# Cross-attention with one matrix for query and key, and the query's constant summed on VectorE

## The chip, the cores and the metric

The kernel runs on one core of a Trainium2 chip. The metric is device time in microseconds (us) of one execution. Of the kernel before, six executions are known.

## What is computed

One pre-norm decoder layer over `x` of 16 sequences x 128 tokens x 256 channels, with a context `ctx_1024` of the same shape, all in float32:

```python
x = x + attn(_layernorm(x), ...)                       # differential attention, 16 heads
x = x + xattn(_layernorm(x), ctx_1024, ctx_1024, ...)  # cross-attention, one head of 256
x = x + ffn(_layernorm(x), ...)                        # 16 routed experts (2 a token) and a shared one

def xattn(q, k, v, Wq, bq, Wk, bk, Wv, bv, Wf, bf):
    qp = q @ Wq.T + bq
    kp = k @ Wk.T + bk
    vp = v @ Wv.T + bv
    attn = softmax((qp / 8.0) @ kp.T)
    return gelu((attn @ vp) @ Wf.T + bf) + v
```

Only the cross-attention is touched by the change.

## The kernel before

A tile holds 128 tokens, that is one sequence, on the 128 partitions. Sequences are numbered by `b` (or `k`), and four of them make a group `g` (512 tokens). The four matrices of the cross-attention come in transposed, `xw["q"]` as `[input, output]`.

**The attention** runs as a software pipeline over the steps `k = 0..20`. Sequence `b` has its score maxima at step `b`, its probabilities at `b + 2`, the two halves of its weighted sum after that (`weigh`, `averaged`), the difference of its two softmaxes at `b + 3`, its RMS norm in `scales` (sum on VectorE, a power on GpSimd, L378, 2.9 us) and `normed` (a product on GpSimd, `o`, L385), and at `b + 5` it is turned on TensorE (`output_turned`, tile `pot`, L394) and projected (`output`, tile `py`, L403). Steps 16 to 20 have no new sequence and only drain the pipeline.

**The cross-attention** is dealt out over the last steps by hand: the dictionary `plan` names for a step `k` and a place 0 to 3 in it the functions that are issued there. What remains of groups 2 and 3 stands in a straight list after the loop, mixed with the layer norms and the routing of the experts and with `next(shared)`, which issues one piece of the shared expert (eight matmul records of 512 columns, 3.44 us). For a group `g` the functions are, in order: `cross_stats` and `cross_normed` (layer norm on VectorE), `turned` (sixteen TensorE transposes: the contexts into `cT`, the normed tokens into `xnT`; and an addition on GpSimd, L661), `queries` and `keys` (the two projections, eight matmul records each, L668; the queries leave PSUM through VectorE at L673, the keys through ScalarE at L678), `softmax` (scores `psc`, L689; their maximum, L694; four exponentials with a sum, L698), `probs_by_key` (`ppt`, L709), `mixes` (`pc`, L718), `finishes` (`pf`, L731; left through VectorE at L737) and `gelu` (with an addition on GpSimd, L746). The value and output weights are made into one matrix beforehand, in `value_weights_turned` and `value_weights`.

**What sets the order.** `in_order` pins the instructions of TensorE, VectorE, ScalarE and GpSimd to the order of the text, each engine for itself. So an engine that waits holds up everything behind it in the text. All PSUM tiles come from one pool of eight banks, in turn: the ninth tile after another waits until the other has been read.

After the cross-attention the router's choice is computed on VectorE (L1035 to L1128), GpSimd scatters the tokens to the experts' slots (`xd`, L1134, 32 indirect DMAs), TensorE goes on with the shared expert meanwhile, and then 36 tiles of routed tokens follow, back to back on TensorE, and at the end the gathers (L1199).

Of the kernel before, what the change touches and what calls it, by code (L numbers as in the profile page):

```python
# [9 lines left out]
F32 = mybir.dt.float32  # L10
AF = mybir.ActivationFunctionType
ALU = mybir.AluOpType
# [7 lines left out]
GB = 4  # L20
# [23 lines left out]
def tile_decoder(  # L44
# [148 lines left out]
    def load(out, in_):  # L193
        pin(nc.sync.dma_start(out=out, in_=in_))
# [7 lines left out]
    with actx:  # L202
# [361 lines left out]

        class cross:
# [19 lines left out]
        def cross_rest():  # L585
            cross.pr = s_tile([P, 3, GB, P], "k30", "x_pr")
            cross.rest, cross.taken = s_tile([P, 16 * D], "qb0", "x_rest"), 0
            cross.cT, cross.mixT = part([P, NC_, GT]), part([P, NC_, GT])
            cross.wv, cross.wvf = part([P, NC_, D]), part([P, NC_, D])
            cross.bvb, cross.bf = part([P, NC_, P]), part([P, D])  # L590
            cross.bq, cross.bk, cross.bv = part([P, NC_]), part([P, NC_]), part([P, NC_])

        def cross_weights():
# [13 lines left out]
            load(out=cross.bf, in_=bf.partition_broadcast(P))  # L607

# [54 lines left out]
        def projected(w, from_t):  # L663
            dst = share.tile([P, NC_, GT], F32, tag=f"{w}T", name=f"{w}T")
            for e in range(NC_):
                pp = bank([P, GT], "pp")
                for c in range(NC_):
                    nc.tensor.matmul(  # L668
                        pp, lhsT=cross.xw[w][:, c, e * P : (e + 1) * P], rhs=from_t[:, c, :],
                        start=(c == 0), stop=(c == NC_ - 1),  # L670
                    )
                if w == "q":
                    nc.vector.tensor_scalar(  # L673
                        dst[:, e, :], pp, cross.bq[:, e : e + 1], 1.0 / TEMPERATURE,
                        ALU.add, ALU.mult,
                    )
                else:
                    nc.scalar.activation(  # L678
                        dst[:, e, :], pp, AF.Identity, bias=cross.bk[:, e : e + 1]
                    )  # L680
            return dst

        def scored(g, qT, kT):
# [9 lines left out]
            nmax = share.tile([P, GB], F32, tag="nmax", name="nmax")  # L693
            nc.vector.tensor_reduce(nmax, psc, AX.X, ALU.max, negate=True)  # L694
            pr = cross.pr[:, g % 2]
            den = share.tile([P, GB], F32, tag="den", name="den")
            for b in range(GB):
                nc.scalar.activation(  # L698
                    pr[:, b, :], psc[:, b, :], AF.Exp, bias=nmax[:, b : b + 1],
# [4 lines left out]
            return pr, rec  # L704
# [43 lines left out]
        def queries(g):  # L748
            cross.qT = projected("q", cross.xnT)

        def keys(g):
            cross.kT = projected("k", cross.cT)

        def softmax(g):
            soft[g] = scored(g, cross.qT, cross.kT)

# [6 lines left out]
        def finishes(g):  # L763
# [17 lines left out]
            (18, 2): [(keys, 1)],  # L781
            (18, 3): [(finishes, 0), (softmax, 1)],
# [3 lines left out]
            (20, 0): [(keys, 2)],  # L786
            (20, 1): [(cross_stats, 3), (finishes, 1), (softmax, 2), (cross_normed, 3)],
# [199 lines left out]
    with sctx:  # L987
# [8 lines left out]
        keys(3)  # L996
# [320 lines left out]
```

## Time and profile before

| | us |
|---|---|
| median of six executions | 632.16 |
| lowest and highest | 628.21, 632.74 |
| the profiled execution: its own time | 631.2 |
| the profiled execution: its span | 629.5 |

The profile shows one execution. PE is TensorE's matmul side, PEld its weight loads, DVE is VectorE, ACT is ScalarE, POOL is GpSimd; L668 is line 668 of the kernel before. A row of a timeline has the start in us from the span's start, the time from the first start to the last end in us, the engine, the line and the operation, and in brackets how long the engine had been idle before and what ended that. One float32 matmul is two records in the trace, one transpose is one. The end of a matmul record is modelled, so the pace of TensorE is read from start to start: 0.43 us for a record of 512 columns, 0.215 us for one of 256, 0.107 us for one of 128 or of 16. PEclk is the clock that TensorE was granted, 1.00 being full speed.

In this execution the cross-attention's first projection starts at 223.3 us, its last piece on TensorE ends at 335.9 us, the scatter runs from 381.8 to 422.5 us, and the routed tiles from 452.9 us.

### The profile page before, as it was taken

What the parts mean: (1) busy time and instruction counts of PE and PEld (TensorE: products, weight loads), DVE (VectorE), ACT (ScalarE), POOL (GpSimd) and SP (SyncE); (2) the same over time, 40 slices, a digit from 0 to 9 for tenths busy, and PEclk for the clock granted to TensorE, in tenths of its full rate; (3) what the DMA queues carried; (4) which work ended last, traced back from release to release, by engine and by line L of the source; (5) the groups of instructions that cost most, each with busy time, mean ns of one, the idle gap of its engine ahead of it and who ended that gap; (6) DMA issues with size and microseconds to landing.
All of it is one profiled execution on the core that took longest, in us unless ns stands there. A gap on an engine that the chain in (4) does not pass through costs nothing. (4 is left out here: it accounts for less than half of the span.)

```text
span 629.5 us, 10681 instructions
## 1 busy us (share of the span) xinstructions
PE 571.8 (91%) x3836; PEld 382.9 (61%) x3836; DVE 304.6 (48%) x694; ACT 211.5 (34%) x476; POOL 182.4 (29%) x159
## 2 busy tenths in 40 slices
PE   2499999999998999988999999648899999999986
PEld 2254564564555656666666674335389999988445
DVE  7683785685677683634545336001132323220543
ACT  2034564665554556243464211000122222220110
POOL 5520062344233442551211005760000000004653
PEclk9589999999998999999999999959999999999999
DMA  3022352421104020005002501220299898812333
GB/s 117 15 95 87 101 208 105 186 102 35 70 3 137 4 77 1 2 0 183 18 2 80 188 0 68 103 97 1 76 329 276 270 286 273 251 43 77 108 109 117
DMA packets 59191, 67.63 MB, mean 107 GB/s; under 512 B 8576, under 2 KB 52096, under 8 KB 59136
## 3 DMA queue, kind: packets, MB, share of 16 engines
q1 hardware_dynamic: 55408, 57.21, 28.0%
q0 software_dynamic: 3072, 8.39, 4.2%
q10 hardware_dynamic: 656, 1.31, 0.6%
q8 instruction: 32, 0.52, 0.3%
q14 instruction: 23, 0.19, 0.1%
HBM read 41.73 MB, written 18.61 MB: 96 GB/s over the span
## 5 line engine op out<-in xcount | busy, mean ns | idle before, releaser
L298 DVE TENSOR_REDUCE nm<-pq 128x4 f32<-128x512 f32 x128 | 79.5, 683 | 42.8 <-PE pq L293 42.7
L1199 POOL DMA_INDIRECT yg<-yd,si x32 | 31.2, 974 | 166.2 <-issue 154.8
L962 PE MATMUL py<-w,h 128*128 128x256 f32 x256 | 59.9, 394 | 17.5 <-DVE h L954 14.3
L330 ACT ACTIVATE pr<-pk 128x384 f32<-128x384 f32 (+1 forms) x192 | 71.5, 463 | 12.5 <-PE pk L324 12.2
L1172 PE MATMUL pu<-xrT,w 128*128 128x128 f32 x576 | 70.2, 275 | 0.0
L1172 PEld LDWEIGHTS pu<-xrT,w 128*128 128x128 f32 x576 | 67.3, 192 | 0.1
L962 PEld LDWEIGHTS py<-w,h 128*128 128x128 f32 x256 | 50.5, 198 | 27.6 <-DVE h L954 15.5
L378 POOL TENSOR_TENSOR rms<-rms,mhalf 128x16 f32<-128x16 f32 x16 | 46.4, 2898 | 64.7 <-DVE rms L377 64.7
L954 DVE TENSOR_TENSOR h<-act,pb 128x512 f32<-128x512 f32 x32 | 21.9, 687 | 87.0 <-PE pb L948 41.2
L953 ACT ACTIVATE act<-pa 128x512 f32<-128x512 f32 x32 | 19.1, 597 | 126.9 <-PE pa L948 87.1
L948 PE MATMUL pa<-xT,w 128*128 128x512 f32 x128 | 60.4, 594 | 0.0
L948 PE MATMUL pb<-xT,w 128*128 128x512 f32 x128 | 60.1, 592 | 0.0
L1179 DVE TENSOR_TENSOR hT<-ract,pu 128x256 f32<-128x256 f32 x36 | 15.2, 421 | 63.8 <-ACT ract L1177 63.8
L324 PE MATMUL pk<-qb,k 32*128 32x384 f32 (+1 forms) x384 | 44.7, 505 | 0.0
L293 PE MATMUL pq<-kb,qT 32*128 32x512 f32 x256 | 44.1, 621 | 0.4 <-DVE a L359 0.4
L1134 POOL DMA_INDIRECT xd<-xn,si x32 | 31.2, 974 | 44.7 <-DVE si L1107 35.2
L948 PEld LDWEIGHTS pb<-xT,w 128*128 128x128 f32 x128 | 24.3, 190 | 30.6 <-issue 30.4
L948 PEld LDWEIGHTS pa<-xT,w 128*128 128x128 f32 x128 | 23.7, 190 | 24.6 <-issue 23.9
L1185 PE MATMUL pyr<-w,hT 128*128 x144 | 37.0, 380 | 0.0
L246 PE MATMUL pp<-xnT,wqk 128*128 128x512 f32 (+1 forms) x64 | 33.9, 655 | 2.3 <-DVE xnT L159 1.4
L341 PE MATMUL po<-pr,v 128*32 128x128 f32 x1024 | 35.5, 280 | 0.0
L1177 ACT ACTIVATE ract<-pu 128x256 f32<-128x256 f32 x36 | 13.8, 384 | 60.1 <-PE pu L1172 60.1
(175 smaller groups left out, 793.8 us busy)
## 6 DMA issues: line engine op xcount, KB each, us to landing
w<-in_L_ffn_routed_w_dram SPq DMA_DIRECT2D x88, 256.0 KB
xd<-zeros SPq DMA_DIRECT2D x11, 512.0 KB
xr<-xd SPq DMA_DIRECT2D x36, 128.0 KB
yd<-yr SPq DMA_DIRECT2D x36, 128.0 KB
w<-in_L_ffn_shared_w_dram SPq DMA_DIRECT2D x12, 256.0 KB
k<-kT SPq DMA_DIRECT2D x32, 64.0 KB
ctx<-in_ctx_dram SPq DMA_DIRECT2D x4, 512.0 KB
x<-in_x_dram SPq DMA_DIRECT2D x3, 512.0 KB
```

The costliest lines, as they stand in the source:

```text
L246: nc.tensor.matmul(pp, lhsT=wqk[:, c, n, e * P : (e + 1) * P], rhs=xnT[:, c, at:], start=(c == 0), stop=(c == NC_ - 1),)
L293: nc.tensor.matmul(pq, lhsT=qT[rows, c, i * P : (i + 1) * P], rhs=kbs[g % 2][rows, c, :, i * P : (i + 1) * P], start=True, stop=True,)
L298: nc.vector.tensor_reduce(nm[:, NM * t + 4 * c : NM * t + 4 * c + 4], pq, AX.X, ALU.max, negate=True)
L324: nc.tensor.matmul(pk, lhsT=k3s[g % 2][rows, k, i * P : (i + 1) * P], rhs=qbs[g % 2][rows, heads, i * P : (i + 1) * P], start=True, stop=True,
L330: nc.scalar.activation(pr[:, 0:n, :], pk, AF.Exp)
L341: nc.tensor.matmul(po[32 * t : 32 * t + 32, j, :], lhsT=vs[g % 2][:, i, 4 * t + j, :], rhs=prs[k][t][:, r, :], start=True, stop=True,)
L378: nc.gpsimd.tensor_tensor(rms, rms, mhalf.to_broadcast([P, H]), ALU.pow)
L948: nc.tensor.matmul(pp, lhsT=w[:, c, fs], rhs=xT[g][:, c, :], start=(c == 0), stop=(c == NC_ - 1),)
L962: nc.tensor.matmul(py[:, i, :], lhsT=hs[u][:, f, b * P : (b + 1) * P], rhs=units[u][2][:, f, :], start=(u == 0 and f == 0), stop=(u == NS ...
L1134: i = nc.gpsimd.indirect_dma_start(out=xd[:, :], out_offset=bass.IndirectOffsetOnAxis(ap=slots[n][:, t : t + 1], axis=0), in_=xns[t // GB] ...
L1172: nc.tensor.matmul(pu[:, n, f, :], lhsT=w12[:, c, n, f * P : (f + 1) * P], rhs=xrT[:, c, :], start=(c == 0), stop=(c == NC_ - 1),)
L1185: nc.tensor.matmul(py, lhsT=hT[:, f, :], rhs=w3[:, bass.ds(e * NC_ + f, 1), :], start=(f == 0), stop=(f == NC_ - 1),)
```

## The change

The scores are `(Wq x + bq) . (Wk c + bk) / 8`. The kernel after multiplies the matrices first: with `Wqk = Wq^T Wk` and `u = Wk^T bq` the part that depends on the context is `(Wqk^T x + u) . c / 8`, so that the scores are taken on the turned contexts `cT` and no keys are projected. What is left, `(x . Wq^T bk + bq . bk) / 8`, is one number for each query; it is computed as a product and sum on VectorE (`cross.same`) and subtracted from the shift of the softmax and added to it again.

- `query_weights_turned` (new, place (15, 3)): eight transposes of `Wq` and `Wk`, two ScalarE evictions of 512 columns, two VectorE products that spread `bk`.
- `query_weights` (new, (16, 1)): the product of the matrices (four matmuls of 256 columns), `u` (four of one column), the vector for the constant (two of 256 columns and two of one), and their evictions.
- `queries` uses `Wqk` and, beside the two evictions, issues four products with a sum over 256 channels and one small addition on VectorE. `queries(0)` and `cross_normed(1)` move from (15, 3) to (16, 3), where `keys(0)` stood.
- `keys` is gone for all four groups. `softmax` of group 1 moves to (18, 2), that of group 2 to (20, 0), that of group 3 to the place of `keys(3)`; `next(shared)` is shifted twice in the list after the loop. `softmax` has two more small operations on VectorE.

```diff
+        def query_weights_turned():
+            cross.wn = {}
+            for n, name in enumerate("qk"):
+                cross.wn[name] = cross.mixT[:, n, :].rearrange("p (m d) -> p m d", m=NC_)
+                pt = bank([P, NC_, D], "pwt")
+                for m in range(NC_):
+                    for c in range(NC_):
+                        nc.tensor.transpose(
+                            pt[:, m, c * P : (c + 1) * P],
+                            cross.xw[name][:, c, m * P : (m + 1) * P], ident,
+                        )
+                nc.scalar.copy(cross.wn[name], pt)
+            for m in range(NC_):
+                nc.vector.tensor_scalar(
+                    cross.bvb[:, m, :], ones, cross.bk[:, m : m + 1], None, ALU.mult
+                )
+
+        def query_weights():
+            wq, wk = cross.wn["q"], cross.wn["k"]
+            pw = bank([P, NC_, D], "pqk")
+            for c in range(NC_):
+                for m in range(NC_):
+                    nc.tensor.matmul(
+                        pw[:, c, :], lhsT=wq[:, m, c * P : (c + 1) * P], rhs=wk[:, m, :],
+                        start=(m == 0), stop=(m == NC_ - 1),
+                    )
+            cross.wqk = cross.xw["q"]
+            nc.scalar.copy(cross.wqk, pw)
+            pu = bank([P, NC_], "pqu")
...
+            nc.vector.tensor_copy(cross.u, pu)
+            pb = bank([P, D + 1], "pqb")
+            for n, rhs in ((slice(0, D), wq), (slice(D, D + 1), cross.bq.unsqueeze(2))):
+                for m in range(NC_):
+                    nc.tensor.matmul(
+                        pb[:, n], lhsT=cross.bvb[:, m, :], rhs=rhs[:, m, :],
+                        start=(m == 0), stop=(m == NC_ - 1),
+                    )
+            nc.scalar.activation(cross.w, pb, AF.Copy, scale=1.0 / TEMPERATURE)
...
+        def queries(g):
+            cross.qT = share.tile([P, NC_, GT], F32, tag="qT", name="qT")
...
+                        pp, lhsT=cross.wqk[:, c, e * P : (e + 1) * P], rhs=cross.xnT[:, c, :],
...
+                nc.vector.tensor_scalar(
+                    cross.qT[:, e, :], pp, cross.u[:, e : e + 1], 1.0 / TEMPERATURE,
+                    ALU.add, ALU.mult,
+                )
+            cross.same = share.tile([P, GB], F32, tag="same", name="same")
+            junk = share.tile([P, NC_, GT], F32, tag="kT", name="junk")
+            for b in range(GB):
+                nc.vector.scalar_tensor_tensor(
+                    junk[:, 0, 0:D], cross.xn[:, b, :], 1.0, cross.w[:, 0:D],
+                    ALU.mult, ALU.mult, accum_out=cross.same[:, b : b + 1],
+                )
+            nc.vector.tensor_scalar(
+                cross.same, cross.same, cross.w[:, D : D + 1], None, ALU.add
+            )
...
-                else:
-                    nc.scalar.activation(
-                        dst[:, e, :], pp, AF.Identity, bias=cross.bk[:, e : e + 1]
-                    )
...
-                        psc[:, b, :], lhsT=qT[:, c, t], rhs=kT[:, c, t],
+                        psc[:, b, :], lhsT=cross.qT[:, c, t], rhs=cross.cT[:, c, t],
...
+            nc.vector.tensor_reduce(shift, psc, AX.X, ALU.max, negate=True)
+            nc.vector.tensor_tensor(shift, shift, cross.same, ALU.subtract)
+            nc.vector.tensor_tensor(shift, shift, cross.same, ALU.add)
...
-            (15, 3): [(queries, 0), (cross_normed, 1)],
-            (16, 1): [(value_weights_turned,)],
+            (15, 3): [(query_weights_turned,)],
+            (16, 1): [(query_weights,), (value_weights_turned,)],
             (16, 2): [(value_weights,)],
-            (16, 3): [(keys, 0)],
+            (16, 3): [(queries, 0), (cross_normed, 1)],
...
-            (18, 2): [(keys, 1)],
-            (18, 3): [(finishes, 0), (softmax, 1)],
+            (18, 2): [(softmax, 1)],
+            (18, 3): [(finishes, 0)],
...
-            (20, 0): [(keys, 2)],
-            (20, 1): [(cross_stats, 3), (finishes, 1), (softmax, 2), (cross_normed, 3)],
+            (20, 0): [(softmax, 2)],
+            (20, 1): [(cross_stats, 3), (finishes, 1), (cross_normed, 3)],
...
-        keys(3)
+        softmax(3)
         routed_to(0)
         experts_stats(1)
         finishes(2)
         experts_normed(1)
-        softmax(3)
+        next(shared)
         routed_turned(1)
-        next(shared)
         probs_by_key(3)
         gelu(2)
+        next(shared)
         routed_to(1)
-        next(shared)
         mixes(3)
```

More of the change, by code (lines that the diff above doesn't have):

```diff
@@ L591, in cross_rest @@
             cross.bq, cross.bk, cross.bv = part([P, NC_]), part([P, NC_]), part([P, NC_])
+            cross.u, cross.w = part([P, NC_]), part([P, D + 1])
         def cross_weights():
@@ L607, in cross_weights @@
             load(out=cross.bf, in_=bf.partition_broadcast(P))
+        def query_weights_turned():
[26 more added lines that the diff above has]
+            pu = bank([P, NC_], "pqu")
+            for c in range(NC_):
+                for m in range(NC_):
+                    nc.tensor.matmul(
+                        pu[:, c : c + 1], lhsT=wk[:, m, c * P : (c + 1) * P],
+                        rhs=cross.bq[:, m : m + 1], start=(m == 0), stop=(m == NC_ - 1),
+                    )
+            nc.vector.tensor_copy(cross.u, pu)
+            pb = bank([P, D + 1], "pqb")
+            for n, rhs in ((slice(0, D), wq), (slice(D, D + 1), cross.bq.unsqueeze(2))):
+                for m in range(NC_):
+                    nc.tensor.matmul(
+                        pb[:, n], lhsT=cross.bvb[:, m, :], rhs=rhs[:, m, :],
+                        start=(m == 0), stop=(m == NC_ - 1),
+                    )
+            nc.scalar.activation(cross.w, pb, AF.Copy, scale=1.0 / TEMPERATURE)
         def value_weights_turned():
@@ L661, in turned @@
             nc.gpsimd.tensor_tensor(xg, xg, cg, ALU.add)
-        def projected(w, from_t):
-            dst = share.tile([P, NC_, GT], F32, tag=f"{w}T", name=f"{w}T")
+        def queries(g):
+            cross.qT = share.tile([P, NC_, GT], F32, tag="qT", name="qT")
             for e in range(NC_):
@@ L668, in projected, with softmax @@
                     nc.tensor.matmul(
-                        pp, lhsT=cross.xw[w][:, c, e * P : (e + 1) * P], rhs=from_t[:, c, :],
+                        pp, lhsT=cross.wqk[:, c, e * P : (e + 1) * P], rhs=cross.xnT[:, c, :],
                         start=(c == 0), stop=(c == NC_ - 1),
                     )
[L672 to L675, printed above, removed]
-                    )
-                else:
-                    nc.scalar.activation(
-                        dst[:, e, :], pp, AF.Identity, bias=cross.bk[:, e : e + 1]
-                    )
-            return dst
-        def scored(g, qT, kT):
+                nc.vector.tensor_scalar(
[11 more added lines that the diff above has]
+                cross.same, cross.same, cross.w[:, D : D + 1], None, ALU.add
+            )
+        def softmax(g):
             psc = bank([P, GB, P], "psc")
@@ L689, in scored @@
                     nc.tensor.matmul(
-                        psc[:, b, :], lhsT=qT[:, c, t], rhs=kT[:, c, t],
+                        psc[:, b, :], lhsT=cross.qT[:, c, t], rhs=cross.cT[:, c, t],
                         start=(c == 0), stop=(c == NC_ - 1),
                     )
-            nmax = share.tile([P, GB], F32, tag="nmax", name="nmax")
-            nc.vector.tensor_reduce(nmax, psc, AX.X, ALU.max, negate=True)
+            shift = share.tile([P, GB], F32, tag="nmax", name="nmax")
+            nc.vector.tensor_reduce(shift, psc, AX.X, ALU.max, negate=True)
+            nc.vector.tensor_tensor(shift, shift, cross.same, ALU.subtract)
+            nc.vector.tensor_tensor(shift, shift, cross.same, ALU.add)
             pr = cross.pr[:, g % 2]
@@ L698, in scored @@
                 nc.scalar.activation(
-                    pr[:, b, :], psc[:, b, :], AF.Exp, bias=nmax[:, b : b + 1],
+                    pr[:, b, :], psc[:, b, :], AF.Exp, bias=shift[:, b : b + 1],
                     accum_out=den[:, b : b + 1],
@@ L703, in scored @@
             nc.vector.reciprocal(rec, den)
-            return pr, rec
+            soft[g] = pr, rec
         def by_key(pr):
@@ L746, in gelu @@
             adds.tensor_tensor(xs[g], xs[g], pre, ALU.add)
[L748 to L755, printed above, removed]
         def probs_by_key(g):
```

## The prediction

> **What bounds the kernel now.** I read the busy times and the 40 slices first, then the chain that ended last, then TensorE's own timeline from 220 to 360 us with the waits in it.
>
> ```profile
> PE 571.8 (91%) x3836; PEld 382.9 (61%) x3836; DVE 304.6 (48%) x694; ACT 211.5 (34%) x476; POOL 182.4 (29%) x159
> PE   2499999999998999988999999648899999999986
> ...
> DVE  7683785685677683634545336001132323220543
> ```
>
> A slice is 15.7 us; the cross-attention lies in slices 14 to 21. TensorE is full there but for two slices; VectorE is at three to six tenths. The chain of waits goes back only to 450 us and is nearly all TensorE; before that TensorE is followed by the shared expert without a break, except for a stretch at 404 to 427 us in which it starves while GpSimd issues the scatter. That scatter hangs on the router, and the router on the last `routed_to`, so it moves along with the cross-attention. So the rule for my sum: **a microsecond that TensorE gains by the end of the cross-attention is a microsecond of the kernel, and one that it spends waiting for a chain on other engines is not gained.** These rows of TensorE's and GpSimd's timelines carry the rest:
>
> ```profile
> 223.32 3.70 PE L668 MATMUL pp<-xnT,xw 128*128 128x512 f32 x8
> ...
> 228.81 0.44 PE L394 MATMUL pot<-ident,o 128*128 128x128 f32 x2 [0.23 <-POOL o L385]
> ...
> 237.50 3.70 PE L668 MATMUL pp<-x_rest,xw 128*128 128x512 f32 x8
> ...
> 281.79 0.69 PE L394 MATMUL pot<-ident,o 128*128 128x128 f32 x2 [1.94 <-POOL o L385]
> 282.26 5.08 PE L668 MATMUL pp<-x_rest,xw 128*128 128x512 f32 x8
> ...
> 296.29 1.74 PE L154 MATMUL pt<-ident,xn 128*128 128x128 f32 x8 [1.96 <-DVE xn L136]
> ...
> 304.92 1.64 PE L154 MATMUL pt<-ident,xn 128*128 128x128 f32 x8 [1.11 <-DVE xn L136]
> 306.40 3.60 PE L668 MATMUL pp<-x_rest,xw 128*128 128x512 f32 x8
> ```
> ```profile
> 273.62 2.90 POOL L378 TENSOR_TENSOR rms<-rms,mhalf 128x16 f32<-128x16 f32 x1 [8.94 <-DVE rms L377]
> 276.48 2.35 POOL L661 TENSOR_TENSOR x<-x,ctx 128x1024 f32<-128x1024 f32 x1
> 278.78 2.37 POOL L746 TENSOR_TENSOR x<-x,ctx 128x1024 f32<-128x1024 f32 x1
> 281.12 0.61 POOL L385 TENSOR_TENSOR o<-o,rms 128x256 f32<-128x256 f32 x1
> ```
>
> TensorE already waits at four places, each time for something that VectorE or GpSimd makes. The projections of 3.5 us are what keeps these waits short: the first is 0.23 us only because `queries(0)` runs ahead of it. The second table is the chain behind the 281.79 row: 8.2 us of GpSimd in a row.
>
> **The work on TensorE.** The four `keys` take 3.54 us (237.50 to 241.04), 3.44 (261.64 to 265.08), 4.92 (282.26 to 287.18) and 3.43 (306.40 to 309.83): 15.3 us off. On come eight transposes, 0.88 us (the eight of the contexts start at 270.53, the next work at 271.41); the product, eight records at 0.215 = 1.72; `u`, eight records of one column at 0.107 (the nearest row, the router's 16 columns, does sixteen in 1.71) = 0.86; the constant's vector, four at 0.215 and four at 0.107 = 1.29. Together 4.75 on, so 10.6 us less. It is not what arrives, and I follow it place by place, "shift" being new minus old time of the same work.
>
> - *At 228.81: shift 0.* In place of `queries(0)` at 223.32 stand 0.88 us of transposes; the work up to the turning of sequence 11 takes 1.7, so TensorE is there at 225.9. `o` is not: GpSimd ends it at 228.75, behind the statistics of group 1 on VectorE, which the change leaves where they were. A wait of 2.9 us. The weights that the transposes need are issued at 218.86 and 219.29, the second 0.43 us behind one that was used at 223.32 without a wait; a late landing would vanish in those 2.9 us.
> - *At 231.95: shift +3.9.* `query_weights` costs 1.72 + 0.86 + 1.29. `queries(0)` then takes the slot of `keys(0)` at equal length.
> - *Step 17: shift +5.2.* VectorE now has, in this slot, the two evictions (1.40), four products with a sum, a small addition (0.1) and `cross_normed(1)` (1.37), and only then reads `pt` of sequence 14. Eight tiles later TensorE needs that bank, 3.8 us after `pt` itself, at 248.8; it gets it at about 250.1. Waiting behind it on TensorE is the rest of step 17.
> - *At 281.79: shift +1.9, although `keys(1)` is gone.* `queries(1)` puts the four sums (2.3 us with the addition) ahead of `rms` of sequence 14, which stood at 259.60: 267.2. From there GpSimd 2.9, `normed` 0.1, the scores' maximum and two small steps 0.9, four exponentials 1.6, reciprocal 0.2, four evictions 1.7: the sum for sequence 15 starts at 274.8, not 272.88, and the 8.9 us from there to `pot` are GpSimd's chain above. It sits idle 2.6 us.
> - *At 296.29: shift -2.8.* `keys(2)` is gone (-4.9), but TensorE meets the wait for `xn(3)`: scores 1.8, maximum and small steps 0.9, exponentials 1.6, reciprocal 0.2, addition 0.4, statistics 2.4, evictions 1.7, first part of `xn` 0.4, from 283.9 on: 293.5.
> - *At 309.83: shift -5.7.* The sums of `queries(3)` delay `xn` of the experts, so the shift at 304.92 is only -2.3; `keys(3)` gives 3.4. From there on both orders hold the same work, and TensorE has no wait up to the scatter.
>
> **The price of a product with a sum.** The trace has none. Below: 0.44 us, the pace of the same operation without a sum (L1205, two in 0.88). Above: 0.89, a product and then a sum over 128x256 as an instruction of its own (L1105, 420 ns, some 0.45 from start to start). I take 0.54, the first row plus the 0.1 at which small VectorE operations follow each other, because on ScalarE the sums of L698 show as a record of their own and the pair still keeps a pace of 0.345 us. Three of the four groups pass it on: 0.1 us on the price is 3 x 4 x 0.1 = 1.2 us.
>
> [...]
>
> **The clock.** A wait also costs what comes after it.
>
> ```profile
> 196.50:199.90 3.40, 1.57 (x9) 0.56 (x7) 3.22 (x11) 1.20 (x5) 0.56 (x1) 1.00 0.59 184
> 199.90:203.30 3.40, 2.71 (x30) 2.29 (x34) 2.90 (x8) 0.37 (x1) 0.64 (x2) 0.50 0.02 5
> 278.40:281.80 3.40, 1.47 (x15) 1.27 (x13) 0.54 (x2) 1.17 (x2) 3.33 (x3) 1.00 0.00 0
> 281.80:285.20 3.40, 3.40 (x6) 1.82 (x7) 0.00 (x0) 0.37 (x1) 0.00 (x0) 0.50 0.00 0
> 292.10:295.50 3.40, 2.22 (x21) 1.98 (x19) 1.17 (x3) 1.29 (x7) 0.01 (x1) 1.00 0.88 274
> ```
>
> In this answer by stretches the second and third columns are the stretch's length and TensorE's busy time, the eighth the granted clock. After 3.4 us with 1.57 or 1.47 us of work the clock was halved, after 2.22 it was not. It made `keys(2)` 4.92 us instead of 3.44: 1.5 us. The new order has waits of 2.9, 2.6 and about 2.5 us where the old one had 0.2, 1.9 and 2.0; whether a wait falls into one stretch or is split over two I can't know. I take one halved stretch more than before: +1.5, with -1.5 and +4.5 as ends.
>
> [...]
>
> **At no cost.** ScalarE loses eight evictions of 687 ns and gets three of some 0.59 and one of 0.4; it is busy for a third of the time, and the shared expert covers it. Two of the three come ahead of `nr`, whose DMA has until step 17. SP's and GpSimd's queues get nothing new. If ScalarE's cover were gone, its price would be at most these 2.2 us.
>
> **The sum**: -5.7 + 1.5 = -4.2 on the profiled execution's 631.2, whose span of 629.5 lies 1.7 below. The median is 1.0 above that execution; I put the same difference on it: 632.2 - 4.2 = **628.0 us**.
>
> **Rivals.**
> - *The gain is used up: no change, 632.* With 0.89 us for the sum the price is 12 x 0.35 = 4.2 us, the whole gain. For it: only the unknown operation has to be dear. Against it: ScalarE's rows.
> - *Slower: half clock at every wait, 637.* Each of the three long waits halves the clock for two stretches, as at 199.9 to 206.7 us, where the loss was about 3.4 us: 3 x 3.4 = 10.2 in place of my 1.5, which gives 636.7. It decides from about five halved stretches more than before. For it: three places with over half of a stretch idle. Against it: two stretches in a row were seen once in this region.
> - *All of it arrives: 621.6.* If the chains on VectorE and GpSimd move with TensorE, the 10.6 us come whole. Against it: the 228.81 row, whose chain does not contain anything that is moved.
>
> **How the numbers follow.** This kernel's runs tell some 0.5% from no change, that is 3.2 us. Forecast 0.50 (own range 624 to 629), all of it 0.04, no change 0.35, slower 0.11. The forecast's low end is 0.44 for the sum (-1.2) and the old clock loss saved (-3.0): 623.8; the high end two halved stretches more and 0.7 for the sum: 628 + 3 + 2 = 633. With part of the no-change case and a little of the slower one the range is 623.5 to 634. Faster 0.54, same 0.35, slower 0.11.
>
> **What would show it.** Right: L394 waits for `o` some 2.9 us near 228.8; no L678; `pot` of sequence 15 near 283.7; the last `mixes` (old 327.19) near 321.5 to 323; VectorE's new rows at 0.5 us. Wrong: if the wait at 228.8 is missing, if the new products take 0.7 us or more, or if the time moves after 360 us, where I have both orders alike.

## The result, and the profile after

| | before | after | ratio after / before |
|---|---|---|---|
| median, us | 632.24 (49 executions) | 636.25 (23 executions, 634.34 to 638.5) | 1.0072, 95% interval 1.0055 to 1.0088 |
| profiled execution, us | 631.2 | 636.89 | |
| its span, us | 629.5 | 635.2 | |

The kernel after is slower by 0.7%. The forecast was 628.0 us with a range of 623.5 to 634.0: the time lies outside it, and on the other side of the kernel before. The ratio is not that of the two medians; in the tables here it lies up to 0.0015 (0.9 us) from it. A time in brackets behind a ratio is worked out from the ratio.

The busy times and the slices of VectorE and of the granted clock, from the page of the kernel after, and as the last line the clock of the kernel before:

```profile
PE 570.2 (90%) x3836; PEld 386.3 (61%) x3836; DVE 316.7 (50%) x741; ACT 207.8 (33%) x472; POOL 182.4 (29%) x159
...
DVE  7685785695675746875555436001123222211443
...
PEclk9589999999988989998899999878899999999999
...
PEclk9589999999998999999999999959999999999999
```

TensorE is busy 1.6 us less than before and not 10.6, VectorE 12.1 us more, and TensorE's clock has an 8 in five slices of the first half after the third, where the page of before has one. So the work that was taken off came back, part of it as the same work at half the pace. TensorE's timeline of the kernel after, rows that answer to those shown of before:

```profile
227.82 0.47 PE L394 MATMUL pot<-ident,o 128*128 128x128 f32 x2 [2.89 <-POOL o L385]
228.22 1.66 PE L324 MATMUL pk<-qb,k 32*128 32x384 f32 x8
229.82 1.95 PE L403 MATMUL py<-wproj,oT 128*128 128x256 f32 x4
...
232.56 1.99 PE L637 MATMUL pqk<-x_rest 128*128 128x256 f32 x8
...
241.95 3.70 PE L720 MATMUL pp<-xnT,xw 128*128 128x512 f32 x8
...
285.44 0.44 PE L394 MATMUL pot<-ident,o 128*128 128x128 f32 x2 [4.36 <-POOL o L385]
285.72 3.25 PE L745 MATMUL psc<-x_rest,qT 128*128 128x128 f32 x16
...
297.87 1.65 PE L154 MATMUL pt<-ident,xn 128*128 128x128 f32 x8 [3.37 <-DVE xn L136]
...
299.82 5.36 PE L720 MATMUL pp<-xnT,xw 128*128 128x512 f32 x8
...
308.44 1.64 PE L154 MATMUL pt<-ident,xn 128*128 128x128 f32 x8 [1.48 <-DVE xn L136]
309.92 3.52 PE L745 MATMUL psc<-x_rest,qT 128*128 128x128 f32 x16
```

The waits for `o` and `xn` are 2.89, 4.36, 3.37 and 1.48 us where they were 0.23, 1.94, 1.96 and 1.11. Behind each of them the next work runs at half clock: behind the first, L324 and L403 take 1.66 and 1.95 us instead of 0.93 and 1.13, and behind the others the scores (L745) take 3.25 and 3.52 us instead of 1.95, the last `queries` 5.36 instead of 3.7.

One measure serves for all kernels below, the **stretch**: from the first of the cross-attention's own work on TensorE (L668 at 223.32 us before, the transposes `pwt` at 222.28 after) to the start of the last `mixes` (`pc`, 327.19 and 329.18). It is 103.87 us before and 106.90 after: +3.0 us. The rest of the 5.7 us between the two profiled executions is an earlier start of the stretch (-1.0) and +3.7 behind the last `mixes`, where both kernels hold the same work. Of the 3.7 us, 2.1 have come by the first turning of routed tokens (`pxt`) and 1.6 come right behind it. The rows of before, then those of after:

```profile
452.91 0.41 PE L1161 MATMUL pxt<-ident,xr 128*128 128x128 f32 x2 [2.42 <-DMA xr<-xd]
453.16 1.88 PE L948 MATMUL pa<-xT,w 128*128 128x512 f32 x4
...
456.95 0.66 PE L1210 MATMUL pxt<-ident,xr 128*128 128x128 f32 x2 [2.42 <-DMA xr<-xd]
457.40 3.28 PE L998 MATMUL pa<-xT,w 128*128 128x512 f32 x4
```

The wait is the same, but after it the clock is halved in the one and not in the other. The mean granted clock from 340 to 480 us is 0.95 before and 0.93 after, and in the kernels below it goes with the time from the last `mixes` to the end: e2 has 0.95 and 302.5 us, as before (302.3); e1, e3 to e7 and e9 have 0.93 and 304.4 to 306.4 us, whatever they do in the cross-attention; on another chip it is 0.99 and 282.4 to 282.6 us in e8 and e10, 1.00 and 280.8 us in e11 and e12. So the 1.6 us are the clock's. The 2.1 us arise where TensorE both starves under the scatter and is granted less (0.80 from 409 to 452 us, 0.85 before), and which of the two makes them is not shown; nor is why one execution is granted less there than another.

**Where the longest wait comes from.** The wait before 285.44 is for `o` of sequence 15. GpSimd's timeline, then VectorE's, of the kernel after:

```profile
278.21 2.35 POOL L712 TENSOR_TENSOR x<-x,ctx 128x1024 f32<-128x1024 f32 x1
280.52 2.53 POOL L805 TENSOR_TENSOR x<-x,ctx 128x1024 f32<-128x1024 f32 x1
284.77 0.62 POOL L385 TENSOR_TENSOR o<-o,rms 128x256 f32<-128x256 f32 x1 [1.72 <-DVE rms L383]
```
```profile
280.01 0.84 DVE L731 SCALAR_TENSOR_TENSOR junk<-xn,x_rest 128x256 f32<-128x256 f32 x1
...
280.89 2.44 DVE L731 SCALAR_TENSOR_TENSOR junk<-xn,x_rest 128x256 f32<-128x256 f32 x1
283.27 0.08 DVE L731 DVE_READ_ACCUMULATOR junk<-xn,x_rest 128x1 f32 x1
283.38 0.42 DVE L731 SCALAR_TENSOR_TENSOR junk<-xn,x_rest 128x256 f32<-128x256 f32 x1
...
284.45 0.17 DVE L383 SCALAR_TENSOR_TENSOR rms<-ss,rms 128x16 f32<-128x16 f32 x1
```

Before, `rms` (L383) was out early, and `o` (L385) followed GpSimd's second addition at once, at 281.12:

```profile
278.77 0.17 DVE L383 SCALAR_TENSOR_TENSOR rms<-ss,rms 128x16 f32<-128x16 f32 x1
```

Now GpSimd is free at 283.05 and waits 1.72 us more for `rms` (L383), which VectorE issues behind the sums of `queries(2)`. The ordinary product with a sum takes 0.42 us and its read-out 0.08, but the second one here takes 2.44: it stands still beside GpSimd's addition of 2.53 us. It starts 0.37 us behind the addition (280.89 against 280.52) and ends 0.28 us behind it (283.33 against 283.05). By what the one holds up the other, no row shows; that they go together e4 shows, which puts the addition later and has no product of group 2 over 0.85 us.

**A second new wait on ScalarE.** From the timelines of ScalarE and VectorE of the kernel after:

```profile
290.17 1.28 ACT L757 ACT_TABLE_LOAD   x1 [3.88 <-DVE nmax L753]
...
293.00 0.18 DVE L762 RECIPROCAL rec<-den 128x4 f32<-128x4 f32 x1 [2.91 <-ACT x_pr L757]
```

Before, the table for the exponential was loaded 5 us ahead of the maximum:

```profile
288.09 1.28 ACT L698 ACT_TABLE_LOAD   x1
```

With the two small steps behind the maximum, the load waits together with the first exponential: 1.28 us more until the reciprocal, and behind that, on VectorE, stand the statistics and `xn` of group 3.

### The profile page after: what moved, and what is told of

Same layout as the page of the kernel before. It is cut to its first block, busy times and chain, and to the rows that moved or that the text cites. A ratio compares the mean times of both kernels' runs of the same rounds, so it can differ in the third digit from the quotient of the medians.

```text
span 635.2 us, 10728 instructions
## 1 busy us (share of the span) xinstructions
PE 570.2 (90%) x3836; PEld 386.3 (61%) x3836; DVE 316.7 (50%) x741; ACT 207.8 (33%) x472; POOL 182.4 (29%) x159
## 5 line engine op out<-in xcount | busy, mean ns | idle before, releaser
L330 ACT ACTIVATE pr<-pk 128x384 f32<-128x384 f32 (+1 forms) x192 | 71.6, 465 | 12.4 <-PE pk L324 12.1
L378 POOL TENSOR_TENSOR rms<-rms,mhalf 128x16 f32<-128x16 f32 x16 | 46.3, 2897 | 64.1 <-DVE rms L377 60.6
L998 PE MATMUL pa<-xT,w 128*128 128x512 f32 x128 | 61.7, 605 | 0.0
L324 PE MATMUL pk<-qb,k 32*128 32x384 f32 (+1 forms) x384 | 45.0, 505 | 0.0
L348 ACT COPY ot<-po 128x512 f32<-128x512 f32 x32 | 18.7, 585 | 49.1 <-PE po L341 49.1
```

Source lines behind the costliest of these rows:

```text
L324: nc.tensor.matmul(pk, lhsT=k3s[g % 2][rows, k, i * P : (i + 1) * P], rhs=qbs[g % 2][rows, heads, i * P : (i + 1) * P], start=True, stop=True,
L330: nc.scalar.activation(pr[:, 0:n, :], pk, AF.Exp)
L378: nc.gpsimd.tensor_tensor(rms, rms, mhalf.to_broadcast([P, H]), ALU.pow)
L998: nc.tensor.matmul(pp, lhsT=w[:, c, fs], rhs=xT[g][:, c, :], start=(c == 0), stop=(c == NC_ - 1),)
```

## The experiments

Every kernel is compared with the kernel before, run beside it on the same chip.

| kernel | median, us | before, us | ratio, 95% interval | stretch, us |
|---|---|---|---|---|
| after | 636.25 | 632.24 | 1.0072 (1.0055 to 1.0088) | 106.90 |
| e1: without sums and steps | 625.76 | 631.11 | 0.9904 (0.9869 to 0.9939) | 95.44 |
| e3: matrices earlier | 633.53 | 631.11 | 1.0038 (1.0011 to 1.0065) | 103.95 |
| e4: first gelu later | 632.77 | 631.11 | 1.0024 (1.0003 to 1.0045) | 103.57 |
| e5: dead work in the waits | 631.45 | 631.11 | 1.0017 (0.9989 to 1.0045) | 103.99 |
| e2: table loaded ahead | 633.04 | 632.44 | 1.0018 (0.9986 to 1.0049) | 103.90 |
| e7: before, with sums and steps | 642.25 | 632.44 | 1.0170 (1.0128 to 1.0213) | 112.54 |
| e9: the repairs of e2, e3, e4 | 630.16 | 632.44 | 0.9960 (0.9931 to 0.9989) | 99.83 |
| e6: e9 without any constant | 621.31 | 632.44 | 0.9839 (0.9799 to 0.9880) | 91.36 |
| e8: without the two steps | 610.68 | 607.23 | 1.0052 (1.0032 to 1.0072) | 104.05 |
| e10: without the products | 604.37 | 607.23 | 0.9947 (0.9930 to 0.9964) | 99.84 |
| e11: sums at the start of softmax | 607.18 | 607.23 | 1.0000 (0.9980 to 1.0020) | 101.91 |
| e12: e9 and e11 together | 600.72 | 607.23 | 0.9879 (0.9850 to 0.9908) | 95.58 |

The last four ran on another chip, on which the kernel before too takes 607.23 us; there, times count only beside that. The kernel after itself was not run on it, so these four stand against it by their ratios, and by the stretch, which starts at the same place there (221.9 to 222.7 us).

**e1, the sums left out.** The sixteen products, the small addition and the two steps on the maximum go; the constant is then missing from the shift of the softmax, where it had been subtracted and added again.

```diff
-            for b in range(GB):
-                nc.vector.scalar_tensor_tensor(
-                    junk[:, 0, 0:D], cross.xn[:, b, :], 1.0, cross.w[:, 0:D],
-                    ALU.mult, ALU.mult, accum_out=cross.same[:, b : b + 1],
-                )
...
-            nc.vector.tensor_tensor(shift, shift, cross.same, ALU.subtract)
-            nc.vector.tensor_tensor(shift, shift, cross.same, ALU.add)
```

> The kernel after without the four products with a sum, their small addition and the two small steps on the shift (the softmax doesn't depend on what they compute). Measure: the stretch from the first row of the cross-attention's weights or queries on TensorE to the start of the last mixes, 103.9 us before, 106.9 after. Theory (chains on VectorE and GpSimd, met without cover, set the pace): the chain to the turning of sequence 15 starts about 2 us earlier, loses the 2.4 us for which one product stood still behind GpSimd's addition, and the experts' first layer norm comes 2 us earlier; the stretch falls to 101 to 103, the time to about 631. Rival (only the halved clock counts, the sums lie beside it): the stretch falls by 1 at most, 635 to 636.

TensorE's and ScalarE's timelines of this kernel:

```profile
280.78 0.44 PE L394 MATMUL pot<-ident,o 128*128 128x128 f32 x2 [1.48 <-POOL o L385]
...
290.17 1.65 PE L154 MATMUL pt<-ident,xn 128*128 128x128 f32 x8 [1.97 <-DVE xn L136]
```
```profile
281.65 1.28 ACT L745 ACT_TABLE_LOAD   x1
283.77 0.37 ACT L745 ACTIVATE x_pr<-psc,nmax 128x128 f32<-128x128 f32 x1 [0.84 <-DVE nmax L741]
```

The waits are down to 1.48 and 1.97 us, the table is there 0.84 us before the maximum, the stretch is 11.5 us shorter, far more than the 4 to 6 that I had expected. So the change is two changes of opposite sign: the product of the matrices brings 5.4 us against before (6.1 by the ratio), and the sums cost some 10.

**e7, the sums alone, in the old order.** The kernel before gets the same products, the small addition and the two steps (on another vector of the same shape; what is subtracted is added again).

```diff
             cross.qT = projected("q", cross.xnT)
+            for b in range(GB):
+                nc.vector.scalar_tensor_tensor(
+                    junk, cross.xn[:, b, :], 1.0, cross.bf,
+                    ALU.mult, ALU.mult, accum_out=cross.same[:, b : b + 1],
+                )
...
+            nc.vector.tensor_tensor(nmax, nmax, cross.same, ALU.subtract)
+            nc.vector.tensor_tensor(nmax, nmax, cross.same, ALU.add)
```

> The kernel before with the sums alone: for each group four products with a sum of xn and the row bf over 256 channels, a small addition, and the two small steps on the softmax's shift, which take away and add the same number. Keys and order are as before, TensorE's work is unchanged. Theory (the sums are dear where no projection on TensorE covers VectorE; in the old order there is cover for groups 0 and 1): 3 to 6 us slower, 635 to 637, stretch 107 to 110. Rival (the sums cost the same anywhere, as much as taking them out of the kernel after gave): 10 us slower, 641 or more. Second rival (they lie wholly beside TensorE): no change.

The time is 9.8 us longer, the stretch 8.7. I had thought that the old order, with the projections of the keys in front of the waits, would hide a part; it hides none. The timelines of TensorE and of VectorE:

```profile
284.23 0.51 PE L394 MATMUL pot<-ident,o 128*128 128x128 f32 x2 [3.87 <-POOL o L385]
284.53 5.27 PE L668 MATMUL pp<-x_rest,xw 128*128 128x512 f32 x8
```
```profile
279.74 2.44 DVE L755 SCALAR_TENSOR_TENSOR junk<-xn,x_rest 128x256 f32<-128x256 f32 x1
```

The same product stands still for the same 2.44 us beside the same addition, and the wait for `o` is nearly as long. The cost of the sums does not come from the new order.

**e8 and e10, which part of the sums costs.** e8 leaves out the two steps on the maximum; e10 fills `same` by one small operation a group in place of the products and keeps the steps.

```diff
 e8
-            nc.vector.tensor_tensor(shift, shift, cross.same, ALU.subtract)
-            nc.vector.tensor_tensor(shift, shift, cross.same, ALU.add)
 e10
-            for b in range(GB):
-                nc.vector.scalar_tensor_tensor(
...
-                cross.same, cross.same, cross.w[:, D : D + 1], None, ALU.add
+                cross.same, cross.w[:, 0:GB], cross.w[:, D : D + 1], None, ALU.add
```

> The kernel after without the two small steps on the maximum (the subtraction and the addition of the constant); the sixteen products with a sum and the small addition stay. Theory A (the steps count for more than their own 0.4 us, because behind them ScalarE loads the table of the exponential only after the maximum has come, 1.28 us): groups 2 and 3 lose 1.7 us each, so some 3 us below the kernel after, a stretch near 103.5 us, and no table load with a wait for the maximum. Rival B (only the 0.4 us a group count, the table load is hidden or stays): at most 1.3 us below the kernel after, a stretch of 105.5 us or more.

> The kernel after without the sixteen products with a sum: the constant of a query is filled in by one small operation a group that stands for it; the two steps on the maximum stay. Theory A: the products carry the larger part, by their 1.9 us a group ahead of the chains and the 2.4 us of one that stands still beside GpSimd's addition: 6 to 8 us below the kernel after, a stretch of 99 to 101 us, the table load still behind the maximum. Rival B (the steps and the table load carry most): at most 4 us below the kernel after, a stretch of 103 us or more. With the run without the steps the two parts should add up to some 10.6 us, the gain of leaving both out; a sum far below that would mean that either of the two alone brings the long waits.

The products carry most. Without them the stretch is 7.1 us shorter than after and the ratio 0.0125 lower (7.6 us); the wait for `o` of sequence 15 falls to 1.83 us. Without the steps the stretch is 2.9 us shorter, as theory A has it, with the table loaded at 286.03 and no wait for the maximum; but the ratio is only 0.0020 lower (1.2 us), and the two intervals overlap. The time thus leaves the share of the steps between 1 and 3 us. The two parts add up to 9.9 of the 11.5 us of e1's stretch, and to 0.0145 of the 0.0168 of its ratio.

**e4, the first gelu later.** GpSimd's addition L805 then comes behind the work that `o` of sequence 15 needs.

```diff
-            (19, 1): [(probs_by_key, 1), (gelu, 0), (queries, 2)],
-            (19, 3): [(mixes, 1)],
+            (19, 1): [(probs_by_key, 1), (queries, 2)],
+            (19, 3): [(mixes, 1), (gelu, 0)],
```

> The kernel after with gelu of group 0 (and its addition on GpSimd) moved from place (19, 1) to (19, 3), behind the product that makes o of sequence 15. Theory (o of sequence 15 comes late because this addition runs ahead of it and keeps one product with a sum on VectorE standing for 2 us): no product over 0.5 us there, o about 2.5 us earlier, the wait at the turning of sequence 15 falls from 4.4 to about 2, the stretch by 2 to 4 with the clock. Rival (the wait is TensorE being early, its cause is further up): the wait shrinks by less than 1 us.

No product of group 2 takes over 0.85 us any more, the wait for `o` falls from 4.36 to 2.34 us, the stretch by 3.3 us, and the ratio from 1.0072 to 1.0024 (3.0 us). That is the standstill (2.0 us of it at the wait) and one halved piece of the clock less (the scores behind the wait take 1.95 us instead of 3.25). The wait for `xn` of group 3 stays at 3.71.

**e2, the exponential's table ahead.** A one-column exponential is issued on ScalarE ahead of `softmax(2)` and `softmax(3)`.

```diff
+        def exp_table():
+            warm = share.tile([P, 1], F32, tag="warm", name="warm")
+            nc.scalar.activation(warm, mhalf, AF.Exp)
...
+            (20, 0): [(exp_table,), (softmax, 2)],
```

> The kernel after with an exponential of one column issued on ScalarE ahead of the softmax of groups 2 and 3, so that ScalarE changes its function table before the scores' maximum is there. In the kernel after the change of table (1.28 us) started only after the maximum, in the kernel before well ahead of it. Theory (the chain maximum, exponentials, reciprocal, addition, statistics, xn(3) is what TensorE waits for in the turning of group 3): xn(3) 1.3 us earlier, the 3.4 us wait there down to about 2.1, the stretch 106.9 down to about 105.5, 635. Rival (ScalarE's table lies beside the path): nothing moves, 106.9.

The table is loaded at 286.84, the first exponential follows the maximum directly at 291.05, and the wait for `xn` of group 3 falls from 3.37 to 1.70 us. Ratio 1.0018 instead of 1.0072 (3.4 us), stretch 3.0 us shorter: twice what I had expected. Its clock was halved in the cross-attention for as long as in after (13.7 us), but at other places. Only 0.7 of the 3.0 us are there at `xn` of group 3; most of the rest stands at the last scores, which ran at full clock (1.95 us instead of 3.52). So this run shows that the load was on the path, but its 3.0 us are not the load's price alone.

**e3, the matrices earlier.** `pqk` and `u` move to place (15, 3), where TensorE waits for `o` of sequence 11; the vector for the constant stays.

```diff
-            (15, 3): [(query_weights_turned,)],
-            (16, 1): [(query_weights,), (value_weights_turned,)],
+            (15, 3): [(query_weights_turned,), (query_weights,)],
+            (16, 1): [(query_constant,), (value_weights_turned,)],
```

> The kernel after with the product of the matrices and u moved from place (16, 1) to (15, 3), ahead of the turning of sequence 11. Theory (the 2.9 us wait for o of sequence 11 is free room on TensorE, and it halves the clock behind it): the wait shrinks below 0.5 us, the clock stays at 1.00 there, the stretch falls by 1.5 (work moved into the wait) to 3 (and the clock): 104 to 105.5, 633 to 635. Rival (the later chains set the end whatever stands here): what is gained here is lost again at the turning of sequence 15, the stretch stays at 106 to 107.

The wait of 2.89 us at 228 is gone (one of 1.23 us, for ScalarE's eviction of `pwt`, has come at 224.53) and with it a halved piece of clock (L324 and L403 take 0.93 and 1.13 us there instead of 1.66 and 1.95); `queries(0)` starts 16.5 us after the transposes `pwt` instead of 19.7. The wait at sequence 15 is 4.36 us again, as if nothing had happened ahead of it, and yet the stretch is 3.0 us shorter and the ratio 0.0034 lower: the chain to it goes along with TensorE.

**e5, dead work in the waits.** Eleven matmuls of 512 columns that nobody reads, 9.5 us of TensorE at full clock, are put in front of the four waits.

```diff
+            for _ in range(n):
+                nc.tensor.matmul(pz, lhsT=ident, rhs=w, start=True, stop=True)
...
+            (15, 3): [(query_weights_turned,), (filler, 3)],
...
+            (19, 3): [(mixes, 1), (filler, 4)],
```

> The kernel after with eleven matmuls of 512 columns added (9.5 us of work on TensorE at full clock) whose result nothing reads: three behind the new transposes, four behind the mixes of group 1, three in the turning of group 3 between contexts and tokens, one ahead of the turning of the experts' first group, that is, into its four waits. Theory (the time that the projections gave free is spent waiting, and the waits halve the clock): the clock stays at 1.00 from 222 to 330 us, the stretch is no longer than after's, 102 to 107, the time 632 to 637. Rival (TensorE's work sets the pace): 9.5 us longer, 646.

TensorE's timeline of this kernel:

```profile
226.70 0.44 PE L394 MATMUL pot<-ident,o 128*128 128x128 f32 x2 [0.31 <-POOL o L385]
...
282.74 0.44 PE L394 MATMUL pot<-ident,o 128*128 128x128 f32 x2 [0.94 <-POOL o L385]
283.01 1.95 PE L747 MATMUL psc<-x_rest,qT 128*128 128x128 f32 x16
...
293.87 1.65 PE L154 MATMUL pt<-ident,xn 128*128 128x128 f32 x8 [1.14 <-DVE xn L136]
...
295.81 3.70 PE L722 MATMUL pp<-xnT,xw 128*128 128x512 f32 x8
```

With 9.5 us more work the kernel is not slower but 3.5 us faster than after (ratio 1.0017 against 1.0072). The waits are 0.31, 0.94, 1.14 and 2.21 us, the scores take 1.95 and the last `queries` 3.70 us, and one piece of the clock is halved in the cross-attention (at 305.2, behind the wait of 2.21) where there were four; I had expected none. This separates two things: TensorE's own time in front of these waits is worth nothing; and the half clock behind the waits costs time by itself.

**e9 and e6, repairs together.** e9 has the edits of e2, e3 and e4. e6 has them too and computes no constant at all: no sums, no steps, no vector for it. Such a constant is the same for all keys of a query and cancels in the softmax, so nothing is lost by that.

```diff
 e6, beside the edits of e2, e3 and e4
-            pb = bank([P, D + 1], "pqb")
...
-            nc.scalar.activation(cross.w, pb, AF.Copy, scale=1.0 / TEMPERATURE)
```

> The kernel after, whole, with three repairs of its order at once: the product of the matrices moved to (15, 3), gelu of group 0 to (19, 3), the table changed early. Alone the first took the stretch from 106.9 to 104.0, the second to 103.6. Theory (each repairs a wait of its own, and what is left are the sums themselves and the clock): they add up, stretch 99 to 101, time 628 to 631, as the prediction had it. Rival (the chains behind take over and the repairs overlap): 102 to 104, no better than the second alone, 632 to 633.

> The three repairs and, besides, no query's constant at all: neither the sums nor the matmuls, the spreading of bk and the eviction for its vector (the softmax doesn't depend on it). Without the sums alone: stretch 95.4, 625.8. Theory: TensorE's 10.6 us less work and 1.3 more that the constant's vector cost arrive but for a wait or two, stretch 90 to 93, 621 to 623. Rival (the waits left in the run without sums are for chains that no longer hold anything of the change): 95 to 96, 625 to 626.

e9 is 0.4% faster than before: a cure of the three side effects turns the change round, but waits of 2.33, 2.43 and 3.07 us stay, for the products still stand ahead of the chains. e6 is 1.6% faster than before, 11.1 us, the best of all versions: in its cross-attention no piece of the clock is halved (1.00 from 220 to 330 us, 0.94 in the kernel after). Between e9 and e6 lie 8.9 us (7.7 by the ratios); the constant's vector, 1.3 us on TensorE, is gone with the sums.

**e11 and e12, the sums at another place.** The four products and the small addition are issued at the start of `softmax`, ahead of the maximum, where VectorE waits for the scores; the normed tokens get a second buffer. e12 adds the repairs of e9.

```diff
-            return share.tile([P, GB, D], F32, tag="xn", name="xn", bufs=1)
+            return share.tile([P, GB, D], F32, tag="xn", name="xn", bufs=2)
...
+            for b in range(GB):
+                nc.vector.scalar_tensor_tensor(
+                    junk[:, 0, 0:D], cross.xns[g][:, b, :], 1.0, cross.w[:, 0:D],
+                    ALU.mult, ALU.mult, accum_out=cross.same[:, b : b + 1],
+                )
...
             shift = share.tile([P, GB], F32, tag="nmax", name="nmax")
```

> The kernel after, with the four products and the small addition of a group issued at the start of its softmax, ahead of the maximum, where VectorE sat idle 4.4 us in group 2 and 2.7 in group 3, and no longer behind the queries; the normed tokens get a second buffer for that. Nothing is left out. Theory A (what counts is the place, ahead of the RMS norm's chain and of the experts' layer norm): it gains nearly what leaving the products out gains, 5 to 8 us below the kernel after, no product above 0.5 us, a stretch of 99 to 102 us. Rival B (the products cost the same wherever they stand): within 2 us of the kernel after, a stretch of 105 us or more.

> The kernel after with the sums at the start of softmax and the three other repairs together (matrices one place earlier, the first gelu of the cross-attention two places later, the exponential's table loaded ahead). Nothing is left out. Theory A: near the version without any constant, which was 11 us below the kernel before, plus the steps on the maximum (0.4 us in three groups), plus the constant's vector (1.3 us on TensorE): 7 to 9 us below the kernel before, a stretch of 93 to 96 us. Rival B (the products cost the same wherever they stand): as the three repairs alone, 2 to 3 us below the kernel before, a stretch near 100 us.

VectorE's timeline of e11:

```profile
280.26 0.60 DVE L383 SCALAR_TENSOR_TENSOR rms<-ss,rms 128x16 f32<-128x16 f32 x1
...
281.23 2.44 DVE L744 SCALAR_TENSOR_TENSOR junk<-xn,x_rest 128x256 f32<-128x256 f32 x1
...
287.08 0.69 DVE L752 TENSOR_REDUCE nmax<-psc 128x4 f32<-128x512 f32 x1 [1.91 <-PE psc L736]
```

In e11 a product still stands still for 2.44 us (I had expected none over 0.5), but `rms` is already out at 280.26, and VectorE has 1.91 us to spare before the scores come. The wait for `o` is still 2.87 us, for GpSimd's two additions stand ahead of it. Ratio 1.0000 against 1.0072 (4.4 us), stretch 5.0 us shorter than after: a little under the 5 to 8 us expected in time, inside the range by the stretch. So the place counts for the greater part of the products' 7.1 us. In e12 the wait for `o` of sequence 15 is 0.39 us (one of 3.38 for `xn` of group 3 stays) and the time 6.5 us below before, against 2.3 in e9; by the ratios 7.3 against 2.5. That is at the low end of the 7 to 9 us expected, with a stretch inside the range (95.58). Rival B falls by both: the same sixteen products cost 4 to 5 us less at another place.

## Why the prediction was wrong

**The step that failed** is "At 281.79: shift +1.9". I followed the four sums of `queries(1)` into the chain of sequence 14 and from there to GpSimd, and wrote that "the 8.9 us from there to `pot` are GpSimd's chain above". The sums of `queries(2)` I did not follow: they stand on VectorE ahead of `rms` of sequence 15 (L383), which before came at 278.77, long before GpSimd asked for it. Now it comes at 284.45, 1.72 us after GpSimd was ready. A second step failed too: "From there on both orders hold the same work" put the time behind the last `mixes` at no change, and it was 3.7 us longer, at a lower granted clock behind 409 us (0.86 up to 480 us, 0.91 before). The table gives forecast and measured times of the same places; the forecast is moved by the 1.04 us by which this execution starts the cross-attention earlier, and leaves out its 1.5 us for the clock.

| place | forecast, us | measured, us | error | what came on |
|---|---|---|---|---|
| `pot` of sequence 15 | 282.65 | 285.44 | 2.8 | 0.9 before GpSimd's chain starts (L378 at 275.36, forecast 274.5); 1.7 wait for `rms` behind the sums of group 2, one of them standing still; 0.2 slower addition |
| `xn` of group 3 | 292.46 | 297.87 | 5.4 | scores at half clock 1.3, table load 1.3 |
| `xn` of the experts | 301.58 | 308.44 | 6.9 | last `queries` at half clock 1.7 |
| last `mixes` | 320.45 | 329.18 | 8.7 | last scores at half clock 1.5 |

The rows on the right add up to 8.6 of the 8.7 us; 1.5 of it was in the sum as the clock's price. The causes at half clock are read from single rows of one execution. With all of that the stretch should have been 4.2 us shorter and was 3.0 longer.

Point by point:
- *The price of a product with a sum* was right: 0.46 us from start to start where nothing is in the way (forecast 0.54). The product itself takes 0.42 us, against 0.48 for L1205 before. No run shows the 0.7 us for the sum in the high end of the range: the runs showed 0.46 us, and 2.44 for a product beside GpSimd's addition. What was wrong is that a price per instruction was taken for the price of the edit. I looked at VectorE's rows alone and not at what GpSimd does at the same time; the trace of before had the additions L661 and L746 at 276.48 to 281.15, right where the sums of `queries(2)` were to stand.
- *Sum of the sums.* By my steps they cost about 6.6 us of the gain (three groups at 2.2 us). Measured by the ratios, with the two steps: 10.6 us in the new order (e1), 10.8 in the old one (e7).
- *The wait at 228.81* came as worked out: 2.89 us against 2.9, and `query_weights` took 3.95 us (forecast 3.87).
- *Step 17*: the shift was about right for a wrong reason. The scores of group 0 start at 250.17 us, 245.72 before: with the earlier start 5.5 us late (forecast 5.2). But no row waits for `pt`'s bank there; in its place stands the half clock behind the wait at 227.82, some 1.6 us.
- *The table of the exponential* is in none of my steps. "Maximum and small steps 0.9" counts the two steps as VectorE work; that they would draw ScalarE's table load behind the maximum I did not see. e2 shows that it was on the path (1.28 us a load; the whole run gained 3.4, with the clock).
- *The clock*: one halved piece more than before was in the sum, three came. In the answer by stretches for the kernel after, the columns are those explained in the prediction:

```profile
224.70:228.10 3.40, 0.51 (x13) 0.20 (x2) 3.16 (x11) 0.58 (x1) 2.26 (x3) 1.00 0.03 6
228.10:231.50 3.40, 3.40 (x14) 1.69 (x12) 0.30 (x2) 1.97 (x5) 2.89 (x1) 0.50 0.00 0
282.70:286.10 3.40, 0.66 (x6) 0.66 (x7) 1.82 (x8) 0.18 (x1) 0.97 (x2) 1.00 0.00 0
286.10:289.50 3.40, 3.40 (x17) 3.31 (x16) 0.50 (x1) 0.19 (x1) 0.00 (x0) 0.50 0.00 0
293.00:296.40 3.40, 1.50 (x11) 1.14 (x10) 3.23 (x13) 0.58 (x1) 0.50 (x1) 1.00 0.94 299
296.40:299.80 3.40, 1.93 (x12) 1.38 (x12) 3.14 (x9) 0.60 (x2) 1.54 (x2) 1.00 1.06 352
299.80:303.20 3.40, 3.40 (x6) 1.51 (x5) 3.23 (x11) 2.32 (x2) 2.33 (x2) 0.50 0.42 132
306.60:310.00 3.40, 1.92 (x13) 1.27 (x12) 2.56 (x11) 0.93 (x3) 0.00 (x0) 1.00 0.00 0
310.00:313.40 3.40, 3.40 (x19) 3.40 (x18) 0.00 (x0) 0.88 (x2) 0.00 (x0) 0.50 0.00 0
```

  Every one of the four long waits was followed by a halved piece, and 1.92 us of work in 3.4 us were not enough to keep the clock. But the busy time alone draws no line: 1.50 us from 293.00 to 296.40 were enough. Each halved piece costs the work behind it 1.3 to 1.7 us. The low end of the range had the old halved piece saved; the kernel after has one behind the same wait (0.50 from 286.10), and e6, without any constant, has none.
- *The gain without the sums* was overrated too. By my steps it should have been some 11 us; e1 shows 5.4 in time and 8.4 in the stretch. A part of TensorE's freed time is wait in e1 as well (1.48 and 1.97 us), and the wait of 2.88 at 227.19 is there unchanged.
- *The rivals.* "Half clock at every wait, 637" gave nearly the measured time by a mechanism that explains only a part: it needed five more halved pieces and 10.2 us from the clock alone; in the cross-attention there were three more, worth some 4.5 us. "The gain is used up" went by a dear product (0.89 us), which it is not. That 10.6 us arrive whole fell at the first wait.
- *What would show it wrong*: I named the time moving after 360 us. It did, by 3.7 us behind the last `mixes`, and the rows show a lower granted clock there; that the change brings it about is not shown, for e2 has the same order there and 302.5 us to the end.
- *Small slips*: two lists of the prediction add up to 0.2 us less than the times written behind them (274.6 for 274.8, 293.3 for 293.5). This changes nothing.

## What to carry to other kernels

An instruction that is put into an engine's fixed order costs what the first waiting chain behind it loses: list every result that stands behind it on that engine, for every copy of the edit (here `rms` of sequence 15 behind the sums of the *third* group, out at 284.45 us and not at 278.77), and look at what the neighbour engine does in the same microseconds. Where TensorE waits anyway, work taken off it brought nothing here (e5, with 9.5 us more, was 3.5 us faster than after), and the longer waits halved the clock of the work behind them, at 1.3 to 1.7 us a piece: fill the waits or shorten their chain first. And before a number is computed cheaply, ask whether it is needed: a query's constant cancels in the softmax, and leaving it out, with its vector, was worth 8 to 9 us.

## What I had not expected of the hardware

- VectorE's product of 0.42 us stood 2.44 us beside a GpSimd addition of 128x1024, in the kernel after and in e2, e3, e7, e8 and e11 alike (2.46 in e5), and GpSimd's addition took 2.53 us in the kernel after and 2.61 in e7 instead of 2.37 before. In e4, e9 and e12, where that addition comes later, no product took over 0.85 us.
- ScalarE's table load of 1.28 us came behind the scores' maximum in the kernel after (290.17, when `nmax` ended 3.88 us of idleness), where two small VectorE steps stand on the operand, and ahead of it without them (281.65 in e1, 286.03 in e8). In the kernel after the exponential follows the load at once (291.46); before, the load came as soon as the eviction ahead of it ended (288.09, the eviction at 288.07). Why the load waits in the one case and not in the other, no run here tells.
- On the other chip, the kernel before takes 25.0 us less (607.23 against 632.24). In e11 the slices of TensorE show no gap under the scatter, where the kernel before has a 6 and a 4:

```profile
PE   2499999999999889997899999999899999999996
```

  From the last `mixes` to the end e11 takes 280.8 us, the kernel before, on the first chip, 302.3. Why TensorE starves there on one chip and not on the other, no run here tells.
